# Attention on one core: small transposes and a 16-row product padded with zeros to 128 x 128 tiles

## The chip, the cores and the metric

The kernel runs on one core of a Trainium2 chip. The metric is the device time of one execution in microseconds, as the median of several runs. The core has a matrix engine (PE, with weight loads shown apart as PEld), a vector engine (DVE), a scalar engine (ACT), a general engine (POOL) and a queue that issues DMAs (SP). All five run on their own and meet at semaphores. "Granted clock" is the share of the full TensorE clock that the throttle let through.

## What is computed

The reference is one transformer block on x of shape (8, 512, 256) in float32: a multi-query attention with a learned "null" key and value, then a delta-rule linear attention, then two mixtures of experts. Only the first part matters here:

```python
xn = ln(x, g_norm)
q = (xn @ Wq).reshape(b, n, 16, 64).transpose(0, 2, 1, 3)
kv = xn @ Wkv                                   # one key and one value head for all 16 query heads
k = concat([null_k, k]); v = concat([null_v, v])
q = l2norm(q) * q_scale; k = l2norm(k) * k_scale
sim = einsum('bhid,bjd->bhij', q, k) * 8 + bias # bias by relative position, and one for the null key
attn = softmax(where(causal and mask, sim, -big))
out = einsum('bhij,bjd->bhid', attn, v)         # (8, 16, 512, 64)
return ln(out.reshape(b, n, 1024) @ Wout, g_out)
```

The null value is the same for every token, so its part of the output is (16 shares of the null key, per token) @ (16 x 256 matrix made once of the null value and Wout).

## The kernel before

The attention runs ahead of the rest. It works through 8 sequences of 4 token tiles (t = 0 to 3) of 128 queries each, so 32 tiles; because of causality, tile t sees (t + 1) x 128 keys. A tile is cut into steps by pairs of heads: `pairs = max(1, 4 // (t + 1))` pairs per step, thus 2 steps for t = 0, 4 for t = 1, and 8 each for t = 2 and 3. The steps of all tiles stand in one list.

For a step k the loop `step(k)` calls, in this order: `attention_weights_turned` of unit k (PE transposes of the exponents, `a_ptp`, copied out by ACT and DVE into `a_pT`), what is due at k - 0.5, `attention_softmax` of unit k + 2 (ACT exponents `a_pr` with their row sums, one accumulator read per head, into `a_rs`), `attention_values` of unit k - 1 (`a_av`), `attention_scores` of unit k + 3 (POOL adds bias and mask into `a_bm`, PE makes `a_s`, DVE adds the two into `a_pr` and finds the minimum `a_mn`), and what is due at k. Steps at other times are put into a table `due` by `at(k, f)`. PE, DVE, ACT and the SP queue are held to program order in this stage; POOL is not: a planner orders its instructions by the times that it expects.

What the change touches, all with tiles of 128 query tokens on the partitions:

- `attention_queries_turned`, half 0, is due at `w.first - 5`; it makes the transposed queries (`a_qtp`, `a_qT`) and allocates the tile's `a_rs` (row sums, then their reciprocals) and `a_pn` (shares of the null key), 128 x 16 each, one column per head.
- `attention_shares` (L531 to L535) is due at `w.half - 2` and `w.last - 2`: POOL subtracts (L531), ACT takes the exponent, POOL adds it to the sums (L533), DVE takes the reciprocal, POOL multiplies (L535). Each call works on the 8 columns of its half.
- `attention_shares_spread` is due at `w.half - 0.5` and `w.last - 0.5`: PE transposes 8 columns of `a_rs` (`a_rp`), ACT copies the 8 x 128 result out (`a_rT`), SP writes it to DRAM and reads it back spread over partitions (`a_rep`).
- `attention_null_turned` is due at `w.last + 1`: PE transposes the 16 columns of `a_pn` (`a_pntp`), ACT copies them out (`a_pnT`).
- `attention_projected` is due at `w.last + 3`: eight products with a 128 x 128 stationary tile, and a ninth, of `a_pnT` (16 x 128) with `a_vw` (16 x 256), add up in `a_op`. L131 and L132 are the helpers that record every matmul and transpose, L125 that of DVE, ACT and SP instructions.
- `a_vw` is made once in `attention_setup` (L287).

`a_rs`, `a_pn` and their like come from a pool with 3 buffers per name. Waits between instructions are drawn automatically, wherever the columns that one writes and another reads overlap.

Of the kernel before, what the change touches and what calls it, by code (L numbers as in the profile page):

```python
# [10 lines left out]
F32 = mybir.dt.float32  # L11
# [7 lines left out]
P = 128  # L19
B, S, D = 8, 512, 256  # L20
NT = S // P
NCT = D // P
H1, DH = 16, 64
# [118 lines left out]
def attention_setup(g, ctx, asides):  # L142
# [4 lines left out]
    nc, tc, ins = g.nc, g.tc, g.ins  # L147
    a = SimpleNamespace(sync=Ordered(tc, nc.sync))
    wp = ctx.enter_context(tc.tile_pool(name="a_w", bufs=1))
# [3 lines left out]
    a.s = ctx.enter_context(tc.tile_pool(name="a_s", bufs=4, space=PSUM))  # L153
    a.bias = wp.tile([P, H1, S], F32, name="a_bias")
    a.ks = wp.tile([P, 1], F32, name="a_ks")
    a.vw = wp.tile([H1, D], F32, name="a_vw")
    by_k = "(c p) n -> p c n"

    with tc.tile_pool(name="as_c", bufs=1) as sp, tc.tile_pool(name="as_w", bufs=2) as wk, tc.tile_pool(
        name="as_ps", bufs=2, space=PSUM  # L160
# [121 lines left out]
        vps = ps.tile([P, 512], F32, tag="ps", name="as_vps")  # L282
        for c in range(8):
            nc.tensor.matmul(
                vps[0:H1, 0:D], nvb[:, c * H1 : (c + 1) * H1], a.wout[:, c, :], start=c == 0, stop=c == 7
            )
        nc.vector.tensor_copy(a.vw, vps[0:H1, 0:D])  # L287

    a.pp = ctx.enter_context(tc.tile_pool(name="a_pp", bufs=4))
    a.tr = ctx.enter_context(tc.tile_pool(name="a_tr", bufs=2, space=PSUM))  # L290
# [134 lines left out]
def attention_queries_turned(g, a, w, half):  # L425

    nc = a.nc
    if half == 0:
        w.qT = a.wk.tile([P, 8, P], F32, tag="qT", name="a_qT")
        w.rs = a.sm.tile([P, H1], F32, tag="rs", name="a_rs")  # L430
        w.mn = a.sm.tile([P, H1], F32, tag="mn", name="a_mn")
        w.pn = a.sm.tile([P, H1], F32, tag="pn", name="a_pn")
        w.avs, w.rep = [None, None], [None, None]
    qf = w.q.rearrange("p h d -> p (h d)")
    tp = a.s.tile([P, 4, P], F32, tag="s", name="a_qtp")
    for i in range(4):
        cc = half * 4 + i
        a.turn(tp[:, i, :], qf[:, cc * P : (cc + 1) * P], g.ident)
    nc.scalar.copy(w.qT[:, half * 4 : half * 4 + 4, :], tp)
# [98 lines left out]
def attention_shares_spread(g, a, w, half):  # L538

    nc = a.nc  # L540
    tp = a.s.tile([P, S], F32, tag="s", name="a_rp")
    a.turn(tp[0:8, 0:P], w.rs[:, half * 8 : half * 8 + 8], g.ident)
    rT = a.sm.tile([8, P], F32, tag="rT", name="a_rT")
    nc.scalar.copy(rT, tp[0:8, 0:P])
    rd = g.dram.tile([8, P], F32, tag="a_rd", name="a_rd", bufs=4)
    nc.sync.dma_start(out=rd, in_=rT)
    w.rep[half] = a.wk.tile([P, 4, P], F32, tag="rep", name="a_rep")
    for i in range(2):
        nc.sync.dma_start(out=w.rep[half][i * DH : (i + 1) * DH], in_=rd[i::2].partition_broadcast(DH))
# [7 lines left out]

def attention_null_turned(g, a, w):
    tp = a.s.tile([P, S], F32, tag="s", name="a_pntp")
    a.turn(tp[0:H1, 0:P], w.pn, g.ident)  # L560
    w.pnT = a.wk.tile([H1, P], F32, tag="pnT", name="a_pnT")
    a.nc.scalar.copy(w.pnT, tp[0:H1, 0:P])


def attention_projected(g, a, w):
# [29 lines left out]
def attention_plan(g, a, asides):  # L595
# [20 lines left out]
    for w in tiles:  # L616
        b, t, s = w.s.b, w.t, w.s
        at(w.half - 2, attention_shares, w, 0)
        at(w.half - 0.5, attention_shares_spread, w, 0)
        at(w.half + 1, attention_divided, w, 0)  # L620
        at(w.last - 2, attention_shares, w, 1)
        at(w.last - 0.5, attention_shares_spread, w, 1)
        at(w.last + 1, attention_divided, w, 1)
        at(w.last + 1, attention_null_turned, w)
        at(w.last + 3, attention_projected, w)
        for half in range(2):
            at(w.first - 9 + half, attention_queries, w, half)
            at(w.first - 7.5 + half, attention_queries_normed, w, half)
            at(w.first - 5 + half, attention_queries_turned, w, half)
        if t == 0:  # L630
            at(w.first - 27, attention_load, s)
            for i in range(NT):
                at(w.first - 25 + i, attention_stats, s, i)
            at(w.first - 21, attention_norm, s)
            at(w.first - 16, attention_turned, s)
            at(w.first - 14, attention_keys, s)
            at(w.first - 10, attention_keys_turned, s)
        at(w.last + 5, attention_out_stats, s, t)
        if t == NT - 1:
            at(w.last + 5, attention_out_norm, s)  # L640
            at(w.last + 8, attention_out, s)
# [1380 lines left out]
@with_exitstack  # L2022
def kernel(ctx: ExitStack, tc: tile.TileContext, ins, out: bass.AP):
    g = start(ctx, tc, ins)
    d = delta_weights(g, ctx)
    m = experts_weights(g, ctx)
    with ExitStack() as part:

        asides = [(60, lambda: delta_loaded(g, d, a)), (68, lambda: delta_made(g, d, a)), (90, lambda: experts_loaded(g, m, a)), (98, lambda: experts_made(g, m, a))]
        asides.append((99, lambda: experts_spread(g, m, a)))  # L2030
        asides += [(71 + 4 * t, lambda t=t: delta_tables(g, d, a, t)) for t in range(NT)]
        asides.append((100, lambda: delta_first_loaded(g, d, a)))
        asides += [(k, lambda f=f: f(a)) for k, f in delta_ahead(g, d)]
        a = attention_setup(g, part, asides)
        a.run(a.last)
    with ExitStack() as part:
        delta_pools(g, d, part)
        experts_pools(g, m, part)
        delta_and_experts(g, d, m, a.outs, out)
# [52 lines left out]
```

## Time and profile before

| | |
|---|---|
| runs, us | 2442.28, 2450.26, 2455.81; median 2450.26 |
| profiled execution: span from first to last instruction, us | 2442.7 (no time outside the span is shown) |
| mean granted TensorE clock | 0.972 |
| busy: PE, PEld, DVE, ACT, POOL, us | 2296.7, 1695.6, 1425.0, 972.9, 1128.1 |
| attention, all but the tail of the last sequence | 0 to about 957 us |
| `a_rp` x64, `a_pntp` x32: median ns of one | 273, 277 |
| `a_op` full, null: median ns of one | 379, 426 |

Engines work side by side, so busy times don't add up. Matmuls are pipelined: the printed duration of one is longer than the distance from its start to the next start, and only the distances add up. In a line of the timeline, the first number is the start, the second the length of the merged group, then engine, source line, operation, output <- inputs, for matmuls rows*columns of the stationary tile, the shape of the moving tile, and the count; brackets tell idle time of the engine before it and who ended it.

### The profile page before, as it was taken

The numbers are of one execution on the slowest core, as the hardware profiler recorded it, in microseconds if no ns is written. First come the engines' busy times: TensorE is split into PE (matmuls) and PEld (weight loads), VectorE is DVE, ScalarE is ACT, GpSimd is POOL, SyncE is SP. The second block draws the span as 40 slices with busy tenths as digits, with TensorE's granted clock in tenths as the row PEclk, the third lists the DMA queues.
The fourth block names the chain that finished last, engine by engine and source line by source line (L and its number), as shares of the span: only waits on it lengthen the run. The fifth ranks groups of instructions, "written<-read, shape, count | busy, mean of one in ns | idle before, by whom it ended". The sixth has DMA issues, their size and how long they took to land.

```text
span 2442.7 us, 57110 instructions
## 1 busy us (share of the span) xinstructions
PE 2296.7 (94%) x22774; PEld 1695.6 (69%) x22774; DVE 1425.0 (58%) x3984; ACT 972.9 (40%) x2652; POOL 1128.1 (46%) x1420
## 2 busy tenths in 40 slices
PE   4899999999999997769899999999999999999999
PEld 2456665565666554557777788888877877888887
DVE  4457667675766675755647457466466466443433
ACT  2657666665766653333233223223222222311111
POOL 3677768677777762343324324225225234232211
PEclk8999999999999998769999999999999999999999
DMA  3201012010111014111323323334235134242433
GB/s 101 61 14 38 32 36 61 27 33 31 37 32 36 19 31 99 53 31 62 69 78 100 84 74 110 78 83 113 73 88 124 48 97 114 58 119 81 118 97 96
DMA packets 345178, 167.23 MB, mean 68 GB/s; under 512 B 193280, under 2 KB 323072, under 8 KB 344912
## 3 DMA queue, kind: packets, MB, share of 16 engines
q1 hardware_dynamic: 341904, 160.16, 24.3%
q8 instruction: 179, 2.93, 0.5%
q10 hardware_dynamic: 3008, 3.43, 0.4%
q14 instruction: 87, 0.71, 0.1%
HBM read 148.33 MB, written 15.18 MB: 67 GB/s over the span
## 4 chain that ended last, share of the span: by engine, by line
PE 44%; DVE 8%; DMA 3%; issue 1%; ACT 1%; POOL 1%; SPq 0%; DVEq 0%; POOLq 0%
PE m_guf L131 12%; PE m_gue L131 8%; PE m_accf L131 6%; PE m_acce L131 4%; PE d_pp L131 3%; DVE d_y L125 2%; PE d_op L131 2%; DMA d_Uh<-d_hU 1%; PE d_cop L131 1%; PE d_uwp L131 1%; DVE d_subst L125 1%; PE d_pw L131 1%; DMA d_hU<-d_V 1%; DVE d_W L125 1%; PE d_sq L131 1%
## 5 line engine op out<-in xcount | busy, mean ns | idle before, releaser
L450 POOL TENSOR_TENSOR a_bm<-a_bias,a_mrow 128x1024 f32<-128x1024 f32 (+1 forms) x176 | 382.1, 2172 | 85.9 <-DVE a_mn L125 72.8
L131 PE MATMUL m_guf<-m_oute,m_wf 128*128 128x256 f32 x1536 | 368.7, 383 | 4.5 <-DVE m_hf L125 2.4
L131 PEld LDWEIGHTS m_guf<-m_oute,m_wf 128*128 128x128 f32 x1536 | 285.0, 190 | 56.0 <-issue 9.1
L131 PE MATMUL m_gue<-m_xT,m_we 128*128 128x256 f32 x1280 | 313.4, 388 | 6.3 <-issue 3.1
L125 DVE CUSTOM_DVE_ANT_0 a_pr<-a_s,a_bm,a_sn 128x512 f32<-128x512 f32 (+3 forms) x512 | 254.2, 545 | 68.6 <-PE a_s L131 52.6
L125 ACT ACTIVATE a_pr<-a_pr,a_mn 128x512 f32<-128x512 f32 (+3 forms) x512 | 282.0, 553 | 17.3 <-DVE a_mn L125 16.7
L125 POOL TENSOR_TENSOR m_hf<-m_hf,m_ctf 128x256 f32<-128x256 f32 x128 | 97.1, 760 | 371.5 <-DVE m_hf L125 183.1
L131 PEld LDWEIGHTS m_gue<-m_xT,m_we 128*128 128x128 f32 x1280 | 237.5, 192 | 42.8 <-DVE m_he L125 5.8
L125 DVE SCALAR_TENSOR_TENSOR m_tf<-m_tf,m_guf 128x256 f32<-128x256 f32 x192 | 80.4, 419 | 291.0 <-ACT m_tf L125 290.5
L125 POOL TENSOR_TENSOR m_he<-m_he,m_cte 128x256 f32<-128x256 f32 x128 | 104.7, 818 | 235.2 <-DVE m_he L125 107.6
L125 ACT ACTIVATE m_tf<-m_guf 128x256 f32<-128x256 f32 x192 | 73.6, 384 | 333.7 <-PE m_guf L131 329.2
L131 PE MATMUL a_s<-a_kT,a_qT 64*128 64x384 f32 (+3 forms) x1024 | 199.4, 471 | 6.7 <-DVE a_mn L125 6.4
L125 DVE TENSOR_TENSOR m_te<-m_gue,m_te 128x256 f32<-128x256 f32 x160 | 67.6, 422 | 234.0 <-ACT m_te L125 234.0
L132 PE MATMUL a_ptp<-table,a_pr 128*128 128x128 f32 x1280 | 179.8, 278 | 20.6 <-DVE a_pT L125 19.2
L131 PE MATMUL m_accf<-m_hf,m_wf 128*128 128x256 f32 x768 | 197.4, 379 | 1.5 <-DVE m_outf L125 1.1
L132 PEld LDWEIGHTS a_ptp<-table,a_pr 128*128 128x128 f32 x1280 | 145.7, 142 | 75.5 <-issue 29.5
L125 ACT ACTIVATE m_te<-m_gue 128x256 f32<-128x256 f32 x160 | 61.4, 383 | 308.8 <-PE m_gue L131 294.8
L131 PE MATMUL a_av<-a_pT,a_kv 128*64 128x256 f32 (+1 forms) x1216 | 166.7, 405 | 3.1 <-DVE a_pT L125 2.9
L131 PE MATMUL m_acce<-m_he,m_we 128*128 128x256 f32 x640 | 163.5, 380 | 0.0
L131 PEld LDWEIGHTS m_accf<-m_hf,m_wf 128*128 128x128 f32 x768 | 145.6, 190 | 22.3 <-issue 1.4
L131 PEld LDWEIGHTS a_s<-a_kT,a_qT 64*128 64x128 f32 x1024 | 83.6, 186 | 81.3 <-issue 39.8
L131 PEld LDWEIGHTS m_acce<-m_he,m_we 128*128 128x128 f32 x640 | 121.3, 190 | 17.0 <-issue 0.3
(351 smaller groups left out, 4114.5 us busy)
## 6 DMA issues: line engine op xcount, KB each, us to landing
a_rep<-a_rd SPq DMA_DIRECT2D x128, 128.0 KB
m_cte<-m_combe SPq DMA_DIRECT2D x64, 256.0 KB
m_ctf<-m_combf SPq DMA_DIRECT2D x128, 128.0 KB
m_we<-in_e_w_gate_dram SPq DMA_DIRECT2D x64, 128.0 KB
m_we<-in_e_w_up_dram SPq DMA_DIRECT2D x64, 128.0 KB
m_we<-in_e_w_down_dram SPq DMA_DIRECT2D x64, 128.0 KB
m_wf<-in_f_gate_w_dram SPq DMA_DIRECT2D x128, 64.0 KB
m_wf<-in_f_up_w_dram SPq DMA_DIRECT2D x128, 64.0 KB
```

Source lines behind the costliest of these rows:

```text
L125: return lambda *args, **kw: tc.keep_in_program_order(f(*args, **kw))
L131: mm = lambda *args, **kw: tc.keep_in_program_order(pe.matmul(*args, **kw))
L132: turn = lambda *args: tc.keep_in_program_order(pe.transpose(*args))
L450: nc.gpsimd.tensor_tensor(bm, a.bias[:, 2 * c0 : 2 * (c0 + pairs), (NT - 1 - t) * P :], s.mrow[:, 0:n].unsqueeze(1).to_broadcast([P, 2 * p ...
```

## The change

The tiles that hold the sums, the null shares and the null value's matrix become 128 columns or 128 rows, with zeros in the new part: `a_rs` is 128 x 136, so that a slice of 128 columns can begin at column 0 or 8; `a_pn` is 128 x 128; `a_vw` is 128 x 256. POOL writes the zeros: once for `a_vw`, and for each of the 32 tiles one MEMSET of 120 columns of `a_rs` and one of 112 columns of `a_pn`, in `attention_queries_turned`. The transposes then take 128 columns in place of 8 and 16, `a_pnT` is copied out at 128 rows in place of 16, and the null value's product runs over 128 rows in place of 16. `a_rT` still takes 8 rows of the transpose.

```diff
-    a.vw = wp.tile([H1, D], F32, name="a_vw")
+    a.vw = wp.tile([P, D], F32, name="a_vw")
+    nc.gpsimd.memset(a.vw, 0.0)
...
-        nc.vector.tensor_copy(a.vw, vps[0:H1, 0:D])
+        nc.vector.tensor_copy(a.vw[0:H1], vps[0:H1, 0:D])
...
     if half == 0:
         w.qT = a.wk.tile([P, 8, P], F32, tag="qT", name="a_qT")
-        w.rs = a.sm.tile([P, H1], F32, tag="rs", name="a_rs")
+        w.rs = a.sm.tile([P, P + 8], F32, tag="rs", name="a_rs")
+        nc.gpsimd.memset(w.rs[:, H1:], 0.0)
         w.mn = a.sm.tile([P, H1], F32, tag="mn", name="a_mn")
-        w.pn = a.sm.tile([P, H1], F32, tag="pn", name="a_pn")
+        w.pn = a.sm.tile([P, P], F32, tag="pn", name="a_pn")
+        nc.gpsimd.memset(w.pn[:, H1:], 0.0)
...
     tp = a.s.tile([P, S], F32, tag="s", name="a_rp")
-    a.turn(tp[0:8, 0:P], w.rs[:, half * 8 : half * 8 + 8], g.ident)
+    a.turn(tp[:, 0:P], w.rs[:, half * 8 : half * 8 + P], g.ident)
...
     tp = a.s.tile([P, S], F32, tag="s", name="a_pntp")
-    a.turn(tp[0:H1, 0:P], w.pn, g.ident)
-    w.pnT = a.wk.tile([H1, P], F32, tag="pnT", name="a_pnT")
-    a.nc.scalar.copy(w.pnT, tp[0:H1, 0:P])
+    a.turn(tp[:, 0:P], w.pn, g.ident)
+    w.pnT = a.wk.tile([P, P], F32, tag="pnT", name="a_pnT")
+    a.nc.scalar.copy(w.pnT, tp[:, 0:P])
```

## The prediction

> **What bounds the kernel now.** I read the busy time by stretch first, then the matmuls around the steps that change, then what ACT and POOL do beside them.
>
> ```profile
> core 0: us, PE busy (x) PEld busy (x) DVE busy (x) ACT busy (x) POOL busy (x), PEclk, DMA share, GB/s
> 0.00:957.00 957.00, 886.94 (x5242) 538.41 (x5242) 609.31 (x1788) 580.53 (x1716) 649.80 (x704) 0.98 0.14 40
> ...
> 301.00:313.00 12.00, 10.96 (x82) 6.92 (x80) 9.62 (x37) 10.66 (x45) 11.59 (x15) 1.00 0.10 29
> 313.00:323.00 10.00, 9.64 (x52) 6.09 (x48) 8.90 (x33) 6.57 (x20) 7.42 (x12) 1.00 0.17 48
> 323.00:406.00 83.00, 82.06 (x485) 50.46 (x486) 49.05 (x131) 51.34 (x141) 58.72 (x60) 1.00 0.21 51
> ```
>
> All that changes lies before 957 us. There one sequence takes about 106 us; in its 83 us for token tiles t = 1 to 3, PE is 99% busy, so a nanosecond saved there counts. In the 12 us where t = 0 runs, POOL (97%) and ACT (89%) are as full as PE. Work after 957 us is untouched, so I carry the difference to the end unchanged.
>
> ```profile
> 352.98 0.81 PE L131 MATMUL a_op<-a_wout,a_oT 128*128 128x256 f32 x3
> 353.72 0.69 PE L131 MATMUL a_op<-a_vw,a_pnT 16*128 16x256 f32 x2
> 354.35 0.76 PE L131 MATMUL a_kp<-a_wkv,a_xnT 128*128 128x144 f32 x4
> ...
> 341.80 0.28 PE L132 MATMUL a_pntp<-table,a_pn 128*16 128x128 f32 x1
> ```
>
> The printed durations overlap; starts tell the cost. Each f32 product is two MATMULs. The last three full ones and the null pair start at 352.98, 353.20, 353.41, 353.72, 354.04, and a_kp's first at 354.35 (narrower windows of this timeline give the starts between). From start to start: full to full 216 ns; the last full one before the 16-row product 309; the two null ones 320 and 305; a_kp's first 227 where its next take 122. So a change of height (16 rows against 128) costs about 90 ns before it and 105 ns after it, and twice that per null product.
>
> ```profile
> 307.07 0.66 PE L132 MATMUL a_ptp<-table,a_pr 128*128 128x128 f32 x4 [0.55 <-DVE a_pT L125]
> 307.56 0.27 PE L132 MATMUL a_rp<-table,a_rs 128*8 128x128 f32 x1
> 307.76 1.95 PE L131 MATMUL a_av<-a_pT,a_kv 128*64 128x256 f32 x16
> ...
> 311.91 0.66 PE L132 MATMUL a_ptp<-table,a_pr 128*128 128x128 f32 x4 [0.49 <-DVE a_pT L125]
> ...
> 314.66 0.70 PE L131 MATMUL a_s<-a_kT,a_qT 64*128 64x256 f32 x4 [0.36 <-DVE a_mn L125]
> ...
> 308.70 0.19 ACT L125 ACTIVATION_READ_ACCUMULATOR a_pr<-a_pr,a_mn 128x1 f32 x1
> 308.79 0.19 ACT L125 ACTIVATE a_pn<-a_pn 128x8 f32<-128x8 f32 x1
> ...
> 310.33 0.21 POOL L533 TENSOR_TENSOR a_rs<-a_rs,a_pn 128x8 f32<-128x8 f32 x1
> 310.49 2.36 POOL L450 TENSOR_TENSOR a_bm<-a_bias,a_mrow 128x1024 f32<-128x1024 f32 x1
> ```
>
> Note that a_rp of t = 0, first half, starts at 307.56, while ACT still writes the second half's exponent sums until 308.89. Note also two PE waits for DVE soon after it, 0.49 and 0.36 us.
>
> **The null product, padded to 128 rows.** It becomes the same form as the eight products before it, so every step is 216. Saved by what follows: a_kp or a_qp, 309+320+305+227 (or 533) becomes 3 x 216 + 122 (or 429), 391 and 390 ns; a_ptp, whose first step falls from 164 to 109, 341 ns; a_pntp, already at 113, 290 ns. The 32 places count 7, 7, 10, 7, and the last, with idle time behind it, at 0.2 us or more: 2.74 + 2.73 + 3.41 + 2.03 + 0.2 = 11.1 us. Two stand among PE idle gaps near the stage's end (930 and 956 us); I take off 0.5: **-10.6 us**.
>
> **The transposes.** a_ptp to a_rp is 109 ns, as a_ptp to a_ptp; a_rp to a_av or a_s is 203 or 202, as a_ptp to these (203). So eight columns gain nothing and 128 lose nothing behind a_ptp, where 63 of 64 stand. But 24 of the 32 a_pntp follow a_s, a change of height, and start the next after 114 ns; full transposes in that place (52 a_qtp) take 165. 24 x 51 ns = **+1.2 us**.
> The Trainium skill (TensorE: Matmul & The Clock Gate, section LDWEIGHTS) puts a weight load at its columns divided by 1.2 GHz whatever its rows. By that the row padding saves nothing and the transposes pay about 0.1 us each, so the sum would be a loss of some 9 us if none were hidden, an estimate from the page alone. The rows above speak against both halves: rows do matter where the height changes, and columns cost only behind such a change.
>
> **The new wait.** The first half's a_rp now reads columns 0 to 127 of a_rs, thus columns 8 to 15, which the exponents of the second half write. Those already issued in program order must end first: heads 8 to 15 at t = 0, 8 to 11 at t = 1, 8 and 9 at t = 2 and 3. Matching each a_rp with that ACT instruction: at t = 2 and 3 ACT is 5.8 to 7.5 us early, at t = 1 1.4 us and more, except in the first sequence, 1.43 us late. At t = 0 ACT ends 1.32 us after a_rp's start in sequences 2 to 7 (308.89 against 307.56), 0.20 in the first, 0.21 early in the last. PE then stands, and queued behind a_rp are a_av and the a_s for later units. Price per t = 0 tile: 1.32 + 0.07 for waking up = 1.39. What is late next: the wait at 311.91 is DVE's (its queue stands behind the reciprocal, that behind POOL L533 at 310.33, that behind POOL's full queue since 295), so PE's lateness swallows 0.49 there and 0.36 at 314.66; ACT's a_rT at 309.36 isn't delayed (a_rp ends at 309.25). Left: 0.54 x 6 = 3.2. The first sequence's t = 0 is covered by a 3.09 us gap at 101.02, its t = 1 (1.5, with gaps of 0.16 and 0.08 behind it) pays 1.3. Sum **+4.5 us**; bounds 0 (all absorbed) and 6 x 1.39 + 0.27 + 1.5 = 10.1. The opposite wait (exponents behind a_rp's read) is no new one: ACT's a_rT copy ahead of them waits for a_rp already.
>
> **The memsets.** MEMSET rows: 128x64 141 ns, 128x128 194, 128x512 514. Two per tile, 120 and 112 columns, about 0.19 + 0.18: 64 add 11.9 us to POOL's 650 of 957, plus 0.3 for a_vw in the setup. POOL is idle 307 us there; the one tight place is 295 to 313, where t = 1's pair is issued: there it moves the DVE wait by 0.37, less than the 0.9 that PE is late by then. Taken at **0**; bounds 0 and 7 x 0.37 = 2.6 if PE were not late. The a_pnT copy (16x128, 253 ns) keeps 128 elements per partition; its reader comes microseconds later: 0, bound 32 x 0.14 = 4.4 us of ACT (a 128x128 exponent takes 0.39), in slack. Extra semaphore waits on 64 a_rp: 0, at most 64 x 0.05 = 3.2 us. A small gain can't be excluded, since POOL isn't held to program order.
>
> **Sum:** -10.6 + 1.2 + 4.5 = -4.9 us on the profiled span of 2442.7, so 2437.8, a factor of 0.9980. The page gives no time outside the span; the span is 0.4 above the fastest run and 7.6 below the median of three, 2450.26. The factor on the median: 2445.4, I say 2445. With the bounds: -9.4 (nothing stalls) to -10.6 + 1.2 + 10.1 + 2.6 = +3.3.
>
> About 0.5% (12 us) is what a measurement of this kernel can tell from no change.
>
> **Rivals.**
> Faster: the stall is absorbed wholly and POOL's new order also closes the DVE-made PE gaps (0.55 + 0.49 + 0.36 + 0.95 around 307 to 366, 2.35 a sequence). For it: POOL order is the planner's, and it plans with the new wait. Against: nothing shortens POOL's work. 7 x 2.35 + 9.4 = 26 at most, half of the gaps gives -18: 2432.
> No saving: the 309, 320 and 305 belong to the null product itself, not to its height. Then +1.2 + 4.5: 2456. Against it: a_kp, a_qp and a_ptp show the same step after any change of height.
> Slower: POOL's queue. The planner orders POOL freely by expected times, and L533 leads a_bm by only 0.16 us at 310.33, less than one memset. If a_bm goes first, L533, the reciprocal, DVE's a_pT copy and PE are 2.36 us later. One such exchange per sequence costs 7 x 2.36 = 16.5 in place of the 4.5: 2457 or so, level at 1.3 us a sequence; beyond 0.5% from some 3.1 us, so from two exchanges (L533 also leads a_bm by 0.33 at 299.60 and 304.51): -9.4 + 33 = +24, 2474. For it: DVE waited 56.3 us for L533 in this stage. Against it: PE-bound tiles have slack for it.
>
> **Chances.** Forecast 0.43, no saving 0.05 (both within 0.5%), faster rival 0.26, slower rival with two exchanges 0.26. The range takes the forecast's bounds and half of each outer rival: 2431 to 2468. The forecast's own range, its bounds on the median (2441 to 2454) with 3 us on either side for the medians' scatter, is 2438 to 2457.
>
> **What would show it.** Right: steps of 216 ns through nine products and none above 250; a_rp at t = 0 starting just after ACT's last accumulator read, with ACT named in its wait; the gaps at 311.91 and 314.66 gone; attention ending some 5 us earlier. Wrong: null steps still over 300, L533 behind a_bm with longer DVE waits for it, or a difference that arises after 957 us.

## The result: slower by 0.7%, and the profile after

The changed kernel took 2466.14 us in the median of 5 runs (2464.43 to 2470.51), against 2450.26 before: ratio 1.0074, 95% interval 1.0057 to 1.0092. A later measurement gave 1.0071 (1.0051 to 1.0090). The profiled execution spans 2462.7 us. The attention's last `a_hn` copy (ACT taking `a_op` out) ends at 968.1 us, where it ended at 957.5.

First the stretches of busy time: the whole attention; then 12 us around t = 0 of the third sequence, the same place as 301 to 313 before; then that place cut in three.

```profile
core 0: us, PE busy (x) PEld busy (x) DVE busy (x) ACT busy (x) POOL busy (x), PEclk, DMA share, GB/s
0.00:968.00 968.00, 882.01 (x5242) 552.83 (x5242) 610.30 (x1788) 581.56 (x1717) 660.44 (x769) 0.97 0.14 40
301.40:313.40 12.00, 8.22 (x54) 5.26 (x52) 9.47 (x37) 9.16 (x39) 11.59 (x16) 0.89 0.08 24
309.00:311.00 2.00, 0.00 (x0) 0.00 (x0) 0.79 (x4) 0.88 (x4) 1.84 (x4) 0.91 0.44 131
311.00:317.00 6.00, 5.60 (x25) 3.09 (x25) 2.80 (x5) 2.23 (x9) 3.04 (x3) 0.50 0.15 44
317.00:323.40 6.40, 6.40 (x44) 3.64 (x42) 5.61 (x21) 3.73 (x14) 4.14 (x9) 0.96 0.15 44
```

PE's busy time in the attention fell from 886.9 to 882.0 us, although the stage became longer. At t = 0, PE lost 2.7 of 11.0 busy microseconds in the 12; from 309 to 311 it does nothing at all, and for the six microseconds after that it runs with a granted clock (third column from the right) of 0.50.

The null product next, in the timeline of PE:

```profile
357.00 1.03 PE L131 MATMUL a_op<-a_wout,a_oT 128*128 128x256 f32 x4
357.86 0.60 PE L131 MATMUL a_op<-a_vw,a_pnT 128*128 128x256 f32 x2
358.30 0.65 PE L131 MATMUL a_kp<-a_wkv,a_xnT 128*128 128x144 f32 x4
```

The pair takes 0.44 us from its first start to the next product's, where it took 0.63. In all 32 places the steps are 215 to 217 ns (but for the very last, with idle time behind it), and the first step of a following `a_kp` is 122 or 123.

Then t = 0 of the third sequence on PE, DVE, POOL and ACT:

```profile
307.51 0.66 PE L132 MATMUL a_ptp<-table,a_pr 128*128 128x128 f32 x4 [0.55 <-DVE a_pT L125]
311.40 0.48 PE L132 MATMUL a_rp<-table,a_rs 128*128 128x128 f32 x1 [3.23 <-DVE a_rs L125]
311.80 3.68 PE L131 MATMUL a_av<-a_pT,a_kv 128*64 128x256 f32 x16
315.42 2.08 PE L131 MATMUL a_s<-a_kT,a_qT 64*128 64x256 f32 x8
...
309.13 0.19 ACT L125 ACTIVATION_READ_ACCUMULATOR a_pr<-a_pr,a_mn 128x1 f32 x1
309.23 0.19 ACT L125 ACTIVATE a_pn<-a_pn 128x8 f32<-128x8 f32 x1
...
308.18 0.19 POOL L432 MEMSET a_rs<- 128x120 f32 x1
308.35 0.25 POOL L411 TENSOR_SCALAR a_rq<-a_rq 128x8 f32<-128x8 f32 x1
308.68 1.67 POOL L696 TENSOR_TENSOR a_rq<-a_rq,table 128x8 f32<-128x8 f32 x1
310.43 0.22 POOL L422 TENSOR_TENSOR a_sn<-a_kv,a_rq 128x16 f32<-128x16 f32 x1
310.73 0.22 POOL L423 TENSOR_TENSOR a_sn<-a_sn,a_nab 128x16 f32<-128x16 f32 x1
310.90 0.20 POOL L536 TENSOR_TENSOR a_rs<-a_rs,a_pn 128x8 f32<-128x8 f32 x1
311.14 0.20 DVE L125 RECIPROCAL a_rs<-a_rs 128x8 f32<-128x8 f32 x1 [1.35 <-POOL a_rs L536]
```

The bracket at `a_rp` names DVE and `a_rs`, not ACT. The first half's transpose waits for the reciprocal of the **second** half's sums. That stands behind L536 (L533 before), which adds the null share; L536 stands in POOL's queue behind a power of 1.67 us and more. The exponents, which the prediction expected to be last, ended at 309.32. In the answer on waits the group reads:

```profile
PE a_rp L132 <- DVE a_rs L125: 29.9, 8, 7.6
```

Eight times, once per sequence: 7.6 us in the first, where it had been 1.8, and 2.5 to 3.7 in the others. In the profile of before, that reciprocal stood at

```profile
310.57 0.20 DVE L125 RECIPROCAL a_rs<-a_rs 128x8 f32<-128x8 f32 x1 [1.20 <-POOL a_rs L533]
```

and thus ended 3.2 us behind the start of `a_rp` at 307.56. Set against before, the start of `a_rp` moves by +3.4 us between t = 3 and t = 0 in most sequences, and in sequences 2 to 7 by another 0.8 to 2.2 up to the second half's; t = 1 gives back 1.9 us, t = 2 and 3 mostly 0.3 to 0.7 each. Apart from the memsets, POOL's order in the attention's sequences is that of before.

### The profile page after: what moved, and what is told of

Its sections match the earlier page's. It is cut to its first block, busy times and chain, and to the rows that moved or that the text cites. A ratio compares the mean times of both kernels' runs of the same rounds, so it can differ in the third digit from the quotient of the medians.

```text
span 2462.7 us, 57218 instructions
## 1 busy us (share of the span) xinstructions
PE 2298.5 (93%) x22774; PEld 1713.9 (70%) x22774; DVE 1427.1 (58%) x3984; ACT 972.8 (40%) x2652; POOL 1138.3 (46%) x1485
## 4 chain that ended last, share of the span: by engine, by line
PE 44%; DVE 8%; DMA 3%; issue 1%; ACT 1%; POOL 1%; SPq 0%; DVEq 0%; POOLq 0%
PE m_guf L131 12%; PE m_gue L131 8%; PE m_accf L131 6%; PE m_acce L131 4%; PE d_pp L131 3%; DVE d_y L125 2%; PE d_op L131 2%; DMA d_Uh<-d_hU 1%; PE d_cop L131 1%; PE d_uwp L131 1%; DVE d_subst L125 1%; PE d_pw L131 1%; DMA d_hU<-d_V 1%; DVE d_W L125 1%; PE d_sq L131 1%
## 5 line engine op out<-in xcount | busy, mean ns | idle before, releaser
L131 PE MATMUL a_av<-a_pT,a_kv 128*64 128x256 f32 (+1 forms) x1216 | 175.3, 423 | 3.0 <-DVE a_pT L125 2.9
```

What stands on the lines that cost most here:

```text
L131: mm = lambda *args, **kw: tc.keep_in_program_order(pe.matmul(*args, **kw))
```

## Experiments

Besides the ratio, one number serves for all: the time per sequence, from the start of the first half's `a_rp` at t = 0 in sequence 2 to that in sequence 7, divided by 5. The start-up, which differs by several microseconds between executions of one kernel, isn't in it. Where a kernel has two profiles, it repeats within 0.2 us; the end of the attention repeats only within 8.

| kernel | ratio to before (95%) | us per sequence | attention ends, us |
|---|---|---|---|
| before, two profiles | 1 | 107.00, 106.91 | 957.5, 951.5 |
| the change, two profiles | 1.0074 (1.0057 to 1.0092), 1.0071 (1.0051 to 1.0090) | 109.45, 109.39 | 968.1, 966.9 |
| null product and shares only, two profiles | 0.9955 (0.9939 to 0.9972) | 105.63, 105.75 | 939.6, 939.0 |
| sums only | 1.0110 (1.0088 to 1.0131) | 110.73 | 976.7 |
| second half's shares later | 0.9990 (0.9978 to 1.0002) | 106.19 | 944.8 |
| halves apart | 0.9959 (0.9945 to 0.9973) | 105.95 | 948.8 |
| wait filled with transposes | 0.9999 (0.9985 to 1.0012) | 106.93 | 951.2 |
| null product only, zeros once, two profiles | 0.9950 (0.9934 to 0.9966) | 105.79, 105.60 | 937.1, 945.1 |
| null product of 64 rows | 0.9999 (0.9984 to 1.0013) | 107.04 | 953.3 |

**Each part alone.** Null product and shares without the sums:

```diff
-        w.rs = a.sm.tile([P, P + 8], F32, tag="rs", name="a_rs")
-        nc.gpsimd.memset(w.rs[:, H1:], 0.0)
+        w.rs = a.sm.tile([P, H1], F32, tag="rs", name="a_rs")
...
-    a.turn(tp[:, 0:P], w.rs[:, half * 8 : half * 8 + P], g.ident)
+    a.turn(tp[0:8, 0:P], w.rs[:, half * 8 : half * 8 + 8], g.ident)
```

> The padded null product and null shares alone (a_vw, a_pn, a_pnT as in the change); the sums a_rs stay 128x16 and their transposes 8 columns wide. Theory (the loss is the wait of the first half's transpose of the sums for the second half's reciprocal at t = 0): no PE wait at a_rp, nine products at 216 ns, attention ends 9 to 10 us before that of the kernel before (its last a_hn copy at 957.1 us), time ratio 0.995 to 0.998. Rival (the memsets, which stand in POOL's queue until a buffer comes free, 21.3 us of waiting at a_pn's after the change): most of the loss stays, attention ends at or after 957 us, ratio 1.000 to 1.006.

Measured: ratio 0.9955, no PE wait at `a_rp` but the 1.8 us that the first sequence had before, 105.63 us per sequence, a gain of 1.3. The attention ends 12 to 18 us ahead of before, where 9 to 10 were foreseen, but 2 to 6 of these lie ahead of the first `a_rp` (91.4 us against 97.0 and 93.5). The memsets of the shares are in this kernel, so they don't carry the loss.

The sums alone (the two edits above in the other direction, on the kernel before):

> The padded sums alone (a_rs 128x136, transposes of 128 columns, its memset); the null product stays 16 rows high. Theory: the whole loss without the gain, PE waits 3.2 us at a_rp in each of 6 sequences and more in the first, attention ends 10.7 + 9.7 = 20 us later than before (at 977 us or so), ratio 1.008 to 1.013. Rival (the null product's padding or its memset carries the loss): ratio within 0.3% of 1.

Measured: ratio 1.0110; the attention ends at 976.7 us. The loss comes with the padded sums. The two parts add up: -1.3 and +3.8 us per sequence make +2.5, which is the change.

**The same width without the overlap.** The second half's sums go to columns 128 to 135, and its slice begins at 32:

```diff
-        w.rs = a.sm.tile([P, P + 8], F32, tag="rs", name="a_rs")
-        nc.gpsimd.memset(w.rs[:, H1:], 0.0)
+        w.rs = a.sm.tile([P, P + 32], F32, tag="rs", name="a_rs")
+        nc.gpsimd.memset(w.rs[:, 8:P], 0.0)
+        nc.gpsimd.memset(w.rs[:, P + 8 :], 0.0)
...
-    a.turn(tp[:, 0:P], w.rs[:, half * 8 : half * 8 + P], g.ident)
+    a.turn(tp[:, 0:P], w.rs[:, half * 32 : half * 32 + P], g.ident)
...
-    nc.scalar.copy(rT, tp[0:8, 0:P])
+    nc.scalar.copy(rT, tp[half * 96 : half * 96 + 8, 0:P])
```

(the exponents, L536 and the reciprocal use the moved columns)

> The whole change with all transposes still 128 columns wide, but the second half's sums in columns 128 to 135 of a 128x160 a_rs, so that the first half's slice (0 to 127) holds none of them; one memset more per tile. Theory: no new wait at all, a_rp at t = 0 starts right behind a_ptp, attention ends 947 to 949 us, ratio 0.995 to 0.998. Rival (128 columns in the transposes, or memsets on POOL, cost the time): ratio 1.003 or more.

Measured: 0.9959. PE at t = 0, third sequence:

```profile
303.65 0.66 PE L132 MATMUL a_ptp<-table,a_pr 128*128 128x128 f32 x4 [0.55 <-DVE a_pT L125]
304.15 0.27 PE L132 MATMUL a_rp<-table,a_rs 128*128 128x128 f32 x1
304.35 1.95 PE L131 MATMUL a_av<-a_pT,a_kv 128*64 128x256 f32 x16
```

The transpose is as wide as in the change, there are more memsets than in the change, and there is no wait and no loss. Neither the width nor the memsets cost it; which columns the slice holds does.

**Only the exponents ahead.** At t = 0 the second half's shares come behind the first half's transpose:

```diff
-        at(w.last - 2, attention_shares, w, 1)
+        at(w.last - 2 if t else w.half - 0.5, attention_shares, w, 1)
```

> The whole change, but at t = 0 the second half's shares (with their reciprocal) are issued behind the first half's transpose of the sums, not ahead of it; then only the exponents stand ahead of it. Theory: the wait at the first half's a_rp falls from 3.2 to the 1.4 us that the prediction named; but the planner now puts the second half's L536 behind one a_bm of 2.36 us, so the second half's a_rp waits 0.5 to 1 us in its place. Attention ends 953 to 959 us, ratio 0.997 to 1.003. Rival (the order of shares doesn't matter, the padded columns or memsets do): 967 us and 1.005 to 1.009, as the change.

Measured: 0.9990, 106.19 us per sequence, attention to 944.8 us, earlier than expected; the second half's `a_rp` was not held up by 0.5 us or more. Here are two sequences of this kernel, in the timeline of PE:

```profile
202.46 0.33 PE L132 MATMUL a_rp<-table,a_rs 128*128 128x128 f32 x1 [1.21 <-ACT a_pr L125]
202.71 1.95 PE L131 MATMUL a_av<-a_pT,a_kv 128*64 128x256 f32 x16
...
306.92 0.33 PE L132 MATMUL a_rp<-table,a_rs 128*128 128x128 f32 x1 [1.21 <-ACT a_pr L125]
307.18 3.06 PE L131 MATMUL a_av<-a_pT,a_kv 128*64 128x256 f32 x16
```

This is the wait that the prediction had named: ACT's exponents, 1.21 us of idle PE, and `a_rp` 1.37 us later than without it. The same 16 products behind it take 1.95 us once and 3.06 us the other time. The stretches of the same profile show why:

```profile
203.00:207.00 4.00, 3.94 (x34) 2.61 (x30) 1.42 (x5) 2.91 (x12) 3.53 (x6) 1.00 0.25 72
307.00:313.00 6.00, 6.00 (x36) 3.65 (x36) 3.33 (x12) 3.27 (x13) 4.52 (x7) 0.72 0.26 75
```

The granted clock (third column from the right) is 1.00 in the first and 0.72 in the second. In sequences 2 to 7 the same wait of 1.21 us brought a stretch of half clock four times, and twice not.

**The wait and the clock taken apart.** The change, with work for PE in the wait:

```diff
+    if w.t == 0 and half == 0:
+        for i in range(24):
+            a.turn(tp[:, P : 2 * P], g.flip, g.ident)
     a.turn(tp[:, 0:P], w.rs[:, half * 8 : half * 8 + P], g.ident)
```

> The whole change, with 24 transposes of constants (24 x 0.109 = 2.6 us) put on PE between a_ptp and the first half's a_rp at t = 0, into unused columns of the same PSUM tile: the wait of 3.2 us stays, PE works through most of it. Theory (besides the wait itself, the idle PE loses half its clock for 3.4 to 6.8 us): no half-clock rows near the t = 0 tiles of sequences 2 to 7, a_rp starts as late as in the change, the 16 a_av behind it take 1.95 us and not 3.68, attention ends 7 to 9 us earlier than in the change (958 to 961 us), ratio 1.002 to 1.006. Rival (the drop of the clock is not due to the wait, or costs nothing): 967 us and 1.006 to 1.009.

```profile
305.56 2.78 PE L132 MATMUL a_rp<-table 128*128 128x128 f32 x24
308.95 0.33 PE L132 MATMUL a_rp<-table,a_rs 128*128 128x128 f32 x1 [0.61 <-DVE a_rs L125]
309.21 1.95 PE L131 MATMUL a_av<-a_pT,a_kv 128*64 128x256 f32 x16
```

```profile
311.00:317.00 6.00, 6.00 (x46) 4.01 (x46) 5.24 (x20) 4.23 (x16) 3.77 (x7) 1.00 0.20 58
```

Measured: 0.9999. `a_rp` still starts only when the reciprocal is there, the clock stays at 1.00, and the `a_av` take 1.95 us, at t = 0 of all the sequences 2 to 8. The sequence takes 106.93 us, against 109.4 in the change and 105.63 (null product and shares only) or 105.95 (halves apart) where there is no wait. So per sequence the wait itself costs 1.0 to 1.3 us, and the change, in which the clock falls, another 2.5. Of these, 1.4 to 2.9 us arise between the two `a_rp` of t = 0 in each of the sequences 2 to 7; in the third PE is never idle there, and up to 317.5 us it has half the clock. `a_rp` starts 3.4 us late at t = 0, but the first one of t = 1 mostly only 1.3 to 1.6: with the clock kept, later waits take in the rest. I had expected 7 to 9 us from the clock in all and a ratio of 1.002 to 1.006; it was about twice that. Useless work on PE made the kernel 0.7% faster than the change.

**Where the height stops to matter.** Zeros written once into two long-lived `a_pnT` tiles, all else as before; once with 128 rows, once with 64 (`P` replaced by 64 in the tiles of `a_vw` and `a_pnT`):

```diff
-    a.vw = wp.tile([H1, D], F32, name="a_vw")
+    a.vw = wp.tile([P, D], F32, name="a_vw")
+    nc.gpsimd.memset(a.vw, 0.0)
+    a.pnTs = [wp.tile([P, P], F32, name=f"a_pnT{i}") for i in range(2)]
+    for x in a.pnTs:
+        nc.gpsimd.memset(x, 0.0)
...
-    w.pnT = a.wk.tile([H1, P], F32, tag="pnT", name="a_pnT")
-    a.nc.scalar.copy(w.pnT, tp[0:H1, 0:P])
+    w.pnT = a.pnTs[w.t % 2]
+    a.nc.scalar.copy(w.pnT[0:H1], tp[0:H1, 0:P])
```

> The kernel before with the null product alone padded to 128 rows: two a_pnT tiles of 128 rows zeroed once in the setup and used in turn, so that neither the shares nor the sums are padded and POOL has no memset per tile. Theory: the gain of the padded product (1.4 us a sequence) without the 1.2 us of the full transposes of the shares and without memsets: attention 1 to 2 us shorter than with the padded null product and shares, ratio 0.993 to 0.996. Rival (the zeros have to travel through the padded transpose to be of use, or the copy into a long-lived tile waits for its last reader): 0.997 to 1.000.

> The same with 64 rows in place of 128, the height of a_s. Theory (what costs is that the height differs from the neighbour's 128 rows): the steps around the null pair stay 309, 320, 305 ns, attention as long as before, ratio 0.998 to 1.002. Rival (any height over 32 rows is as good, or the cost falls with the rows): steps at or near 216 ns, ratio 0.994 to 0.997.

With 128 rows: 0.9950, the lowest ratio of all, though its interval overlaps that of the padded null product and shares; the difference between these two isn't settled, and by their two profiles they take the same 105.7 us per sequence. The 1 to 2 us that I had expected between them don't show. With 64 rows: 0.9999. The timeline of the latter:

```profile
349.84 1.03 PE L131 MATMUL a_op<-a_wout,a_oT 128*128 128x256 f32 x4
350.79 0.70 PE L131 MATMUL a_op<-a_vw,a_pnT 64*128 64x256 f32 x2
351.42 0.76 PE L131 MATMUL a_kp<-a_wkv,a_xnT 128*128 128x144 f32 x4
```

Steps of 309, 320 and 307 ns: 64 rows cost as much as 16. A low height by itself costs nothing more: in before, the `a_s` of 64 rows and 256 columns start in pairs 7 ns apart, and 209 ns later comes the next pair. What costs is being of another height than the neighbours.

**What follows the attention.** From the end of the last `a_hn` copy to the end of the span the first profile of before took 1485.2 us, that of the change 1494.5, though the code there is the same.

> The kernel before once more, unchanged, for a second profile. From the last a_hn copy to the end its first profile took 1485.2 us, those of the five others, whose code there is the same, 1490.5 to 1495.0. Theory (the first profile was short there by chance): 1488 to 1496 us. Rival (the change lengthens what follows the attention): 1484 to 1487 us.

> The change once more, unchanged. Ratio 1.005 to 1.009. From the last a_hn copy to the end its first profile took 1494.5 us, the two profiles of the kernel before 1485.2 and 1483.6. If that stretch is longer by the program: 1493 to 1496 us again, and the loss beyond the 10.7 us of the attention is its part. If it varies from one execution to the next: anywhere from 1483 to 1496 us.

> The padded null product with zeros written once, a second profile. That stretch took 1485.8 us in its first. By the program: 1485 to 1487 us again. By chance: anywhere from 1483 to 1496 us.

> The padded null product and shares, a second profile. That stretch took 1492.2 us in its first. By the program: 1491 to 1493.5 us again. By chance: anywhere from 1483 to 1496 us.

Measured: before 1483.6; the change 1491.5; zeros once 1491.6, where it had been 1485.8; null product and shares 1491.5, where it had been 1492.2. My expectation for the kernel before was wrong. One program differs by 6 us from one execution to the next (zeros once), so two profiles each can't settle whether the change lengthens this stretch. The attention ends at 967.5 us in the mean of the change's two profiles and at 954.5 in that of before, 13.0 us apart; the medians differ by 16 (2466.1 - 2450.3; in the later measurement 2461.2 - 2445.4). The two can't be set off against each other: the profiled executions of before were 7 to 8 us faster than the medians of their measurements, those of the change 1 to 2, and the end of the attention differs by 8 us between the two profiles of zeros once. How much of the loss arises behind the attention, if any, stays open.

## Why the prediction was wrong

- **The null product: right.** All steps fell to 216. A gain of 10.6 us over 8 sequences less 1.2 for the transposes is 1.2 per sequence; the two parts without the sums gave 1.3.
- **The transposes: right.** Behind `a_ptp` the 128 columns cost nothing; the kernel with the halves apart shows it. A full `a_pntp` behind `a_s` takes 164 ns to the next start, foreseen 165.
- **The new wait: this step failed.** I found that the first half's slice now holds columns 8 to 15, and looked only for the exponents that write them ahead of `a_rp`. But `attention_shares` of the second half writes them too, by L533 and by the reciprocal. It is due at `w.last - 2`, the first half's transpose at `w.half - 0.5`. At t = 0 `w.last` is `w.half + 1`, so the shares come first in program order; at t = 1 to 3 they come later, and there no wait arose in sequences 2 to 8. In the first, t = 1 waited 1.32 us for the exponents, as foreseen. The two dates stand in the code, and the prediction itself shows L533 writing `a_rs` at 310.33, 2.8 us behind the start of `a_rp`. PE waited 3.23 us and `a_rp` started 3.4 us late, where the sum had 1.32 and 1.39.
- **What swallows it: right in kind, and more than foreseen as long as the clock holds.** PE did arrive late at the two DVE-made gaps of 0.49 and 0.36 us, and they are gone. With the wait filled, some 2 us of the 3.4 were made good, where the sum had 0.85; in the change the half clock took that back.
- **The clock: a term missing from the sum.** The profile of before showed half-clock stretches in this stage after PE gaps of 1.7, 2.6 and 2.2 us (at 472, 851 and 919 us), and the sum let PE stand idle without asking for it. Wait and clock together cost 3.5 to 3.8 us per sequence (1.0 to 1.3 for the wait, 2.5 with the clock, from the filled wait), where the sum had 0.54. The 1.39 us named for the exponents' wait were well sized (measured 1.37, with the shares moved). Of these, against null product and shares only, 0.4 us were left at the first `a_rp` of t = 1 in the two sequences that kept the clock, and 1.2 in the four that lost it; so even for the wait that it named, the 0.54 was too low wherever the clock fell. With that wait alone, the change measured 0.9990, its interval just reaching 1.
- **The memsets: nearly right.** The one at 308.18 us put off L536 by about 0.1 us. They also stood in POOL's queue until a buffer came free (21.3 us in all for `a_pn`, 9.3 for `a_rs`), a wait that the prediction had not listed. It follows PE's lateness: with the halves apart the memsets of `a_pn` waited 0.4 us in all, those of `a_rs` 4.8.
- **The rivals.** The slower one had the right sign and the wrong mechanism: POOL exchanged nothing. It did lie on the same chain (POOL, reciprocal), which I priced for a disorder but not for a direct wait. The range, 2431 to 2468, held the time only through that rival; the forecast's own, 2438 to 2457, did not.

## What to carry to other kernels

Before a read is widened, list every instruction that writes the added columns and stands ahead in program order, with the dates of the plan worked out for the shortest tile, and follow each to what it waits for itself. A wait on a full matrix engine is to be priced with the clock that it loses behind it: here that was some twice the wait's own cost. A small product between larger ones is worth padding to their height (0.5% here, with the zeros written once or for each tile), if no other reader is drawn in.

## What the runs showed of the hardware

- A change of the stationary tile's height between 128 rows and 16 or 64 made the last step ahead of it 89 to 93 ns longer (309 and 305 against 216) and the first step behind it 104 or 105 (320 against 216, 227 against 122), for f32 products. Where the first one behind it was a transposition, that was 55 ns with 128 columns (164 against 109) and 4 or 5 with 16 (113 or 114 against 109). Away from such a change, 8 columns took the same time as 128 (109 ns from `a_ptp`, 202 or 203 to the next product).
- An idle PE of 1.21 us at one place (0.66 us of work behind an idle 0.55, which alone brought none there in before) brought half clock for 3.4 us in four of six sequences, one of 3.23 us brought 3.4 or 6.8 us; the 16 products behind it then took up to 3.7 us in place of 1.95. I had not expected this from 1.2 us.
- Transposes of constants, 2.8 us of them, with 0.6 us of idle PE left, were enough to keep the clock at 1.00 there.
